# Convolution weights in two pools, the last stores of each convolution phase on ScalarE's queue, and the last two output tiles in pieces

## The chip, the cores and the metric

The kernel runs on one core of one Trainium2 chip. The metric is the device time of one execution in microseconds (us); the median of several runs counts. Single durations come from one profiled execution.

## The reference

The input x has 8 images of 256 channels of 56 x 56, float32. Two layers follow each other, each added to its own input:

```
x = x + involution(gn(x))          # layer 0: a 7x7 kernel per pixel and group, made from the pixel itself
x = x + tri_block(gn(x))           # layer 1

def tri_block(x):
    out1 = relu(batch_norm(conv3x3(x, ternary(w1))))
    out2 = batch_norm(conv3x3(out1, ternary(w2)))
    return relu(out1 + out2)
```

`gn` is a group norm. `ternary` turns a weight into -1, 0 or 1 by two thresholds, and the convolution counts its centre tap twice. `batch_norm` uses mean and variance over all 8 images, so nothing can be normalised until the last image's convolution is done.

## The kernel before

The work runs in four stages, one after the other, with all large intermediates in DRAM.

- **Layer 0** (to about 1180 us) computes the involution and stores its result x1 to DRAM (`x1_d`). It also turns the two weight tensors into ternary, transformed ones (`wq_d`). Its instructions are held in the order of the text by `pin`.
- **Phase 1** (`conv_phase(1, ...)`, to about 1615 us) computes the first convolution from x1 and stores its raw result to `y1_d`.
- **Phase 2** (`conv_phase(2, ...)`, to about 2060 us) normalises y1, applies Relu, computes the second convolution and stores its raw result to `y2_d`.
- **The final stage** (lines 1017 to 1037) reads y1, y2 and x1 again and writes relu(relu(bn(y1)) + bn(y2)) + x1.

A convolution phase loops over n = 0 to 15: an image b = n // 2 and its upper or lower half. The two-dimensional convolution is a one-dimensional transform along rows: `transform` makes six planes (k = 0 to 5) from four-row groups, each plane is multiplied by its own weights `wq[k]`, and the six products are combined to four rows. The planes are worked on in the order `ORDER = (1, 2, 3, 4, 0, 5)`, each with 24 matmuls (line 461), 12 for either half of the output channels. The input half n is loaded by `load` into two `raw` tiles (line 311), normalised into the padded buffer `xp`, and transformed through temporaries in the pool `tmpp` (tags `ta`, `tr`). VectorE writes the four rows of the result into `y`; the stores at line 501 wait for the last of them. ScalarE sums y and its square for the batch norm (line 416, with `dummy` as a place for the unused output); in the last half these sums are made in three parts as rows get ready (`last_rows`), and their results go through `batch_norm_params`, a chain of small VectorE instructions with one Sqrt on ScalarE. `weights(i, k)` loads one of the six weight tiles of 6144 bytes per partition; phase 1 gets all six before its loop, those of phase 2 follow in the last half of phase 1, each after the last matmul with its predecessor in the same place.

The final stage works on 16 tiles j (image b, half of the channels t), each of 128 partitions x 3136. For each it loads y1f, y2f and x1f on SP's queue (line 1026), and runs Relu on ScalarE (L1033), y2 times scale plus that on VectorE (L1034), Relu on ScalarE (L1035), and the addition of x1 on VectorE (L1036); ScalarE's queue stores the result (L1037). y1f_0 means the tile of y1 with j = 0. A name has two or three homes, and the load of y1f_2 waits until the home of y1f_0 is no longer read:

```
fa, fb, fc = ...                                     # three pools, one after the other in memory
homes = {"y1": (fc, fa), "y2": (fc, fb), "x1": (fc, fb, fb)}
```

The pools of the final stage lie where those of the convolution phases lay, in the same order from the start: `rawp` (12,992 bytes per partition), `wqp` (36,864), `pad` (14,848), `tmpp` (25,984), and others. `fa` (12,544) covers the raw tiles, `fb` (37,632) the end of the raw tiles, the weights and the first bytes of `pad`, and `fc` (37,632) covers `pad` and part of `tmpp`. A load may start when the last reader of what lay in its home's place is done.

Outside layer 0, the order of the instructions on each engine and queue is chosen when the kernel is built, by a planner: among the instructions that it takes for ready, the one that is earlier in the text goes first. On the chip, each queue is worked in that order, and an instruction that must wait holds up those behind it.

Of the kernel before, what the change touches and what calls it, by code (L numbers as in the profile page):

```python
# [8 lines left out]
F32 = mybir.dt.float32  # L9
F32R = mybir.dt.float32r  # L10
# [5 lines left out]
SBUF = bass.MemoryType.SB  # L16

P = 128
B, C, H, W = 8, 256, 56, 56
HW = H * W  # L20
CT = C // P
# [50 lines left out]
NH = HR * W  # L72
# [4 lines left out]
ORDER = (1, 2, 3, 4, 0, 5)  # L77
# [10 lines left out]
def involution_tri_block_kernel(  # L88
# [3 lines left out]
    nc = tc.nc  # L92
    out = out.rearrange("b c h w -> b c (h w)")
# [9 lines left out]
    x1_d, y1_d, y2_d = scratch("x1d"), scratch("y1d"), scratch("y2d")  # L103
# [191 lines left out]

    def weights(i, k):

        w = wqp.tile([P, CT, 3, C], F32R, tag=f"wq{k}", name=f"wq{i}_{k}")
        n = CT * 3 * C
        nc.sync.dma_start(w.rearrange("p t k o -> p (t k o)").bitcast(F32),  # L300
                          wq_d[i - 1][:, SLOT[k] * n:(SLOT[k] + 1) * n])
        return w

    def load(i, n, src_d):

        b, h = n // 2, n % 2
        raws = []
        for t in range(CT):
            raw = rawp.tile([P, RAW * W], F32, tag=f"raw{t}", name=f"raw{i}_{n}_{t}")
            r0 = h * (H - RAW)  # L310
            nc.sync.dma_start(raw, src_d[b][t][:, r0 * W:(r0 + RAW) * W])
            raws.append(raw)
        return raws

    def conv_phase(i, begun, src_d, norm, stats, shift, dst_d, follow):
# [6 lines left out]
        wq, raws = begun  # L322
# [104 lines left out]
        nxt, begun = {}, ({}, None)  # L427
        for _ in transform(0, raws, nxt):
            pass
        raws = load(i, 1, src_d)  # L430
        for n in range(2 * B):
            b, h = n // 2, n % 2
            cur, nxt = nxt, {}
            more = n + 1 < 2 * B
            steps = transform(n + 1, raws, nxt) if more else iter(())
            next(steps, None)
            final = n == 2 * B - 1
            if n + 2 < 2 * B:
                raws = load(i, n + 2, src_d)
            elif not final and follow:  # L440
                begun = {}, load(i + 1, 0, dst_d)
            y = wk.tile([P, CT, NH], F32, tag="y", bufs=2, name=f"y{i}_{n}")
            yr = [y.rearrange("p o (r k w) -> p o k r w", k=4, w=W)[:, :, k] for k in range(4)]

            def row_of(k, x, c, z, op):
                for to in range(CT):
                    nc.vector.scalar_tensor_tensor(yr[k][:, to], x[:, to], c, z[:, to],
                                                   ALU.mult, op)

            def half(name):  # L450
                return wk.tile([P, CT, HT, W], F32, tag=name, name=f"{name}{i}_{n}")

            m = {}
            for k in ORDER:
                ps = ps_c.tile([P, CT, 512], F32, tag="conv", name=f"c{i}_{n}_{k}")
                for to in range(CT):
                    c, last = 0, CT * 3 * 2 - 1
                    for part in cur[k]:
                        for t in range(CT):
                            for dx in range(3):  # L460
                                nc.tensor.matmul(  # L461
                                    ps[:, to, :NM], wq[k][:, t, dx, to * P:(to + 1) * P],
                                    part[:, t, :, dx:dx + W], start=(c == 0), stop=(c == last))
                                c += 1
                if final and follow:
                    begun[0][k] = weights(i + 1, k)
                m[k] = ps[:, :, :NM].rearrange("p o (r w) -> p o r w", w=W)
                next(done, None)
                if k in (2, 4):
                    e = half("e")  # L470
                    nc.scalar.copy(e, m[k])
                if k == 2:
                    s, d = half("s"), half("d")
                    nc.vector.tensor_tensor(s, m[1], e, ALU.add)
                    nc.vector.tensor_tensor(d, m[1], e, ALU.subtract)
                elif k == 4:

                    s2, d2 = half("s2"), half("d2")
                    nc.vector.tensor_tensor(s2, m[3], e, ALU.add)
                    nc.vector.tensor_tensor(d2, m[3], e, ALU.subtract)  # L480
                    nc.vector.tensor_tensor(yr[1], d2, d, ALU.subtract)  # L481
                    row_of(2, s2, 2.0, s, ALU.subtract)
                    for z, z2, c in ((s, s2, 0.5), (d, d2, 4.0)):
                        flat, flat2 = (v.rearrange("p o r w -> p (o r w)") for v in (z, z2))
                        nc.vector.scalar_tensor_tensor(flat, flat2, c, flat,
                                                       ALU.mult, ALU.subtract)
                    if final:
                        last_rows(n, y, 1, 2)
                elif k == 0:
                    row_of(0, m[0], 1.5, s, ALU.add)  # L490
                    if final:
                        last_rows(n + 1, y, 0, 1)
                elif k == 5:
                    row_of(3, m[5], 6.0, d, ALU.add)
                    if final:
                        last_rows(n + 2, y, 3, 1)
                next(steps, None)
            for _ in steps:
                pass
            for to in range(CT):  # L500
                nc.sync.dma_start(dst_d[b][to][:, h * NH:(h + 1) * NH], y[:, to])
            done = statistics(n, y)
        return begun

# [472 lines left out]


    with ExitStack() as ph2:
        rawp, wqp, pad, tmpp, planes, wk, ps_c = (  # L980
            ph2.enter_context(tc.tile_pool(name=name, bufs=bufs, space=space))
            for name, bufs, space in (
                ("rawp", 1, SBUF), ("wqp", 1, SBUF), ("pad", 1, SBUF), ("tmpp", 1, SBUF),
                ("planes", 8, SBUF), ("wk", 1, SBUF), ("ps_c", 4, PSUM)))

        def norm_x1(dst, src, b, t, engine):
            bias, scale = gn2[:, b, t, 1:2], gn2[:, b, t, 0:1]
            if engine is nc.scalar:
                nc.scalar.activation(dst, src, AF.Identity, bias=bias, scale=scale)
            else:  # L990
                nc.vector.tensor_scalar(dst, src, scale, bias, ALU.mult, ALU.add)

        begun = load(1, 0, x1_d)
        begun = {k: weights(1, k) for k in ORDER}, begun

        xp = pad.tile([P, 4, CT, HT + 1, WP], F32, tag="xp", name="xp")
        nc.gpsimd.memset(xp, 0.0)
        begun = conv_phase(1, begun, x1_d, norm_x1, st1, nc1, y1_d, True)

        sc1, bi1 = batch_norm_params(st1, nc1, g1_sb, b1_sb, "bn1")

        def norm_y1(dst, src, b, t, engine):
            bias, scale = bi1[:, t:t + 1], sc1[:, t:t + 1]
            if engine is nc.scalar:
                nc.scalar.activation(dst, src, AF.Relu, bias=bias, scale=scale)
            else:
                nc.vector.tensor_scalar(dst, src, scale, bias, ALU.mult, ALU.add)
                nc.vector.tensor_scalar(dst, dst, 0.0, None, ALU.max)  # L1010

        conv_phase(2, begun, y1_d, norm_y1, st2, nc2, y2_d, False)
# [3 lines left out]
    sc2, bi2 = batch_norm_params(st2, nc2, g2_sb, b2_sb, "bn2")  # L1016
    with ExitStack() as ph4:

        fa, fb, fc = (ph4.enter_context(tc.tile_pool(name=name, bufs=1))
                      for name in ("fa", "fb", "fc"))  # L1020
        homes = {"y1": (fc, fa), "y2": (fc, fb), "x1": (fc, fb, fb)}

        def loaded_image(name, j, src):
            k = j % len(homes[name])
            v = homes[name][k].tile([P, HW], F32, tag=f"{name}{k}", name=f"{name}f_{j}")
            nc.sync.dma_start(v, src)
            return v

        for b in range(B):
            for t in range(CT):  # L1030
                y1, y2, x1 = (loaded_image(name, b * CT + t, src[b][t])
                              for name, src in (("y1", y1_d), ("y2", y2_d), ("x1", x1_d)))
                nc.scalar.activation(y1, y1, AF.Relu, bias=bi1[:, t:t + 1], scale=sc1[:, t:t + 1])  # L1033
                nc.vector.scalar_tensor_tensor(y1, y2, sc2[:, t:t + 1], y1, ALU.mult, ALU.add)  # L1034
                nc.scalar.activation(y1, y1, AF.Relu, bias=bi2[:, t:t + 1])  # L1035
                nc.vector.tensor_tensor(x1, x1, y1, ALU.add)  # L1036
                nc.scalar.dma_start(out[b, t * P:(t + 1) * P, :], x1)  # L1037


# [69 lines left out]
```

## Time and profile before

| | us |
|---|---|
| median of 3 runs | 2310.3 |
| lowest and highest run | 2309.58, 2313.76 |
| the profiled execution | 2306.55 |
| its span, from first to last instruction | 2304.8 |

| engine | busy us | share of the span |
|---|---|---|
| PE (matmul) | 1872.9 | 81% |
| VectorE (DVE) | 1720.3 | 75% |
| ScalarE (ACT) | 1266.5 | 55% |
| GpSimd (POOL) | 589.4 | 26% |

The DMA engines moved 412.81 MB, 179 GB/s over the span. The busy shares are averages over stages with different limits, so they don't say what a change in one stage is worth; that is read from the stage itself. In the answers shown below, a timeline line has the start in us, the duration, the engine (SPq and ACTq are the DMA issues of SP and ScalarE), the line in the code, the operation, what is written from what, and how often; in square brackets stands how long the engine had been idle before, and which instruction ended that. A line of windows has the stretch and its length, then the busy time of PE, of PE's weight load, of DVE, ACT and POOL with the number of instructions in brackets, the granted PE clock, the busy share of the 16 DMA engines, and the GB/s that they moved.

### The profile page before, as it was taken

What the parts mean: (1) busy time and instruction counts of PE and PEld (TensorE: products, weight loads), DVE (VectorE), ACT (ScalarE), POOL (GpSimd) and SP (SyncE); (2) the same over time, 40 slices, a digit from 0 to 9 for tenths busy, and PEclk for the clock granted to TensorE, in tenths of its full rate; (3) what the DMA queues carried; (4) which work ended last, traced back from release to release, by engine and by line L of the source; (5) the groups of instructions that cost most, each with busy time, mean ns of one, the idle gap of its engine ahead of it and who ended that gap; (6) DMA issues with size and microseconds to landing.
All of it is one profiled execution on the core that took longest, in us unless ns stands there. A gap on an engine that the chain in (4) does not pass through costs nothing.

```text
span 2304.8 us, 72684 instructions
## 1 busy us (share of the span) xinstructions
PE 1872.9 (81%) x31088; PEld 1721.3 (75%) x31088; DVE 1720.3 (75%) x2898; ACT 1266.5 (55%) x2453; POOL 589.4 (26%) x1320
## 2 busy tenths in 40 slices
PE   5879888987988988999979999999799999970000
PEld 4767777776777777778779999999799999970000
DVE  3666867767677685765679999998899999964444
ACT  2545455455454555556546666665576666663433
POOL 3535555454454554646410000000000000000000
PEclk9989999999999999999989999999899999985555
DMA  4635657466465564735463333334333333359998
GB/s 156 198 106 175 190 143 211 145 183 189 118 202 160 173 202 137 212 118 166 138 235 114 114 115 130 139 131 154 122 137 126 114 114 114 130 222 398 426 430 377
DMA packets 159391, 412.81 MB, mean 179 GB/s; under 512 B 55518, under 2 KB 66140, under 8 KB 150876
## 3 DMA queue, kind: packets, MB, share of 16 engines
q1 hardware_dynamic: 154624, 381.35, 49.1%
q10 hardware_dynamic: 4444, 26.81, 2.8%
q8 instruction: 245, 4.01, 0.7%
q14 instruction: 78, 0.64, 0.1%
HBM read 264.05 MB, written 144.05 MB: 177 GB/s over the span
## 4 chain that ended last, share of the span: by engine, by line
PE 54%; DMA 9%; DVE 7%; ACT 3%; issue 2%; SPq 0%; POOL 0%; DVEq 0%; ACTq 0%; POOLq 0%
PE c L461 36%; PE pg L770 8%; PE pa L803 5%; DMA x1f<-x1d 4%; DMA y1f<-y1d 2%; PE ptq L737 2%; DVE a L779 2%; DMA out_y<-x1f 2%; PE pk L639 2%; PE pt L705 1%; DVE x1f L1036 1%; ACT a L774 1%; DVE inv L816 0%; DMA piece_w<-in_w 0%; DVE y1f L1034 0%
## 5 line engine op out<-in xcount | busy, mean ns | idle before, releaser
L461 PE MATMUL c<-pl,wq 128*128 128x392 f32 x4608 | 858.2, 348 | 22.0 <-ACT pl L351 20.3
L461 PEld LDWEIGHTS c<-pl,wq 128*128 128x128 f32 x4608 | 855.3, 190 | 24.7 <-ACT pl L351 20.7
L779 DVE TENSOR_TENSOR a<-pg,bt 126x756 f32<-126x756 f32 (+3 forms) x640 | 392.1, 654 | 182.2 <-ACT a L774 125.6
L770 PE MATMUL pg<-kr,wl 64*126 64x140 f32 (+1 forms) x6144 | 459.4, 293 | 53.7 <-DVE a L779 51.8
L770 PEld LDWEIGHTS pg<-kr,wl 64*126 64x126 f32 x6144 | 395.0, 195 | 107.8 <-issue 48.4
L803 PE MATMUL pa<-a,q 126*32 126x48 f32 x17920 | 276.0, 210 | 54.5 <-DVE a L779 28.7
L803 PEld LDWEIGHTS pa<-a,q 126*32 126x32 f32 x17920 | 227.0, 113 | 103.7 <-issue 34.8
L774 ACT ACTIVATE a<-pg,bt 126x126 f32<-126x126 f32 x768 | 244.0, 476 | 103.2 <-PE pg L770 103.2
L819 POOL TENSOR_TENSOR x<-x,inv 128x168 f32<-128x168 f32 x320 | 172.6, 540 | 472.7 <-DVE inv L816 394.1
L816 DVE SCALAR_TENSOR_TENSOR inv<-pa,half_sb,inv 128x168 f32<-128x168 f32 x320 | 117.0, 366 | 180.8 <-ACT inv L815 158.7
L351 ACT CAST pl<-r 128x812 fp32r<-128x812 f32 x192 | 162.4, 867 | 142.9 <-DVE r L346 126.7
L740 ACT COPY q<-ptq 126x384 f32<-126x384 f32 x320 | 139.2, 482 | 162.1 <-issue 89.8
L331 POOL MEMSET xp<- 128x116 f32 x32 | 6.3, 197 | 832.3 <-DVE a L346 832.3
L416 ACT ACTIVATE dummy<-y,nc 128x1568 f32<-128x1568 f32 (+2 forms) x144 | 210.1, 1459 | 5.3 <-DVE y L481 3.5
L352 DVE TENSOR_TENSOR pl<-r,pl 128x812 fp32r<-128x812 f32 x192 | 186.8, 999 | 29.9 <-ACT pl L351 28.8
L662 POOL TENSOR_SCALAR xn<-x,gn 128x224 f32<-128x224 f32 (+2 forms) x384 | 175.0, 476 | 117.7 <-PE pt L705 65.6
L662 POOL TENSOR_SCALAR xe<-x,gn 128x168 f32<-128x168 f32 (+2 forms) x384 | 164.8, 448 | 0.0
L737 PE MATMUL ptq<-ident_sb,xe 128*126 128x128 f32 x960 | 148.6, 292 | 1.8 <-issue 0.9
L708 ACT COPY stg<-pt 98x512 f32<-98x512 f32 x128 | 75.4, 589 | 132.6 <-issue 96.2
L149 DVE BATCH_NORM_STATS2 st<-x 128x6 f32<-128x392 f32 x256 | 138.0, 555 | 12.0 <-DMA x<-in_x 10.4
L815 ACT ACTIVATE inv<-pa,half_sb 128x168 f32<-128x168 f32 x320 | 128.5, 402 | 27.5 <-PE pa L803 24.8
L737 PEld LDWEIGHTS ptq<-ident_sb,xe 128*126 128x126 f32 x960 | 107.1, 145 | 16.8 <-issue 2.4
(144 smaller groups left out, 1826.3 us busy)
## 6 DMA issues: line engine op xcount, KB each, us to landing
q<-xtd SPq DMA_DIRECT2D x320, 252.0 KB
raw<-x1d SPq DMA_DIRECT2D x32, 812.0 KB
raw<-y1d SPq DMA_DIRECT2D x32, 812.0 KB
x<-in_x SPq DMA_DIRECT2D x64, 392.0 KB
xtd<-stg SPq DMA_DIRECT2D x128, 196.0 KB
x1d<-x SPq DMA_DIRECT2D x64, 392.0 KB
y1d<-y SPq DMA_DIRECT2D x32, 784.0 KB
y2d<-y SPq DMA_DIRECT2D x32, 784.0 KB
```

What stands on the lines that cost most here:

```text
L351: nc.scalar.copy(hi, r)
L352: nc.vector.tensor_tensor(lo, r, hi.bitcast(F32), ALU.subtract)
L416: nc.scalar.activation(dst, v, f, bias=shift[:, to:to + 1], accum_out=stats[:, to, j, n:n + 1])
L461: nc.tensor.matmul(ps[:, to, :NM], wq[k][:, t, dx, to * P:(to + 1) * P], part[:, t, :, dx:dx + W], start=(c == 0), stop=(c == last))
L662: nc.gpsimd.tensor_scalar(dst[:, i - d - k0:f - d - k0, :, x0:x0 + n], v[:, i:f, :, j0:j0 + n], scale, bias, ALU.mult, ALU.add)
L737: nc.tensor.transpose(pt[:NQ, k * P:(k + 1) * P], xe[c % 2][:, k, PY * ty:PY * ty + QY].rearrange("p r x -> p (r x)"), ident_sb)
L740: nc.scalar.copy(loads[b, c, ty][:NQ, NK:].rearrange("p k c -> p (k c)"), pt[:NQ, :NX * P])
L770: nc.tensor.matmul(dst, wl[rows, c, gp, o:o + NQ], kr[py][rows, px, :], start=True, stop=True)
L774: nc.scalar.activation(whole[:, g0 + i, p0 + j], ps[:NQ, i, j * nt:(j + 1) * nt], AF.Identity, bias=bt[:, c, g0 + i, p0 + j:p0 + j + 1])
L779: nc.vector.tensor_tensor(dst[:, g0:g0 + 2, p0:p0 + nv].rearrange("q g p t -> q g t p"), ps[:NQ, :, t0 * nv:t1 * nv].rearrange("q i (t p) ...
L803: nc.tensor.matmul(ps[o:o + 32, k * 2 * n:(k + 1) * 2 * n], q[:NQ, k, o:o + 32], av[:, t + k, g * 2 * n:(g + 1) * 2 * n], start=True, stop ...
L819: nc.gpsimd.tensor_tensor(xv, xv, iv.rearrange("p t (y x) -> p y t x", x=PX), ALU.add)
```

## The change

- The pool of the weights, `wqp`, becomes two: `wqa` for k = 1, 2, 3, 4 and `wqb` for k = 0, 5. A tile of 64 bytes per partition, `space`, is put ahead of the raw tiles, so that `wqa` ends at byte 37,632.
- Before the loop of phase 1 only the weights of k = 1, 2, 3 are asked for with the first raw tiles; those of 4, 0, 5 follow after the raw tiles of n = 1.
- In the last half of either phase (`final`), the two stores of y are issued on ScalarE's queue instead of SP's.
- The final stage has four pools: `fa` (12,544 bytes, over the raw tiles), `fb` (25,088, over the end of the raw tiles and `wqa`), `fc` (12,544, over `wqb` and the first bytes of `pad`), `fd` (37,632, at the addresses that `fc` had). y1f lives in fd and fa, y2f in fd and fb, x1f in fd, fb and fc.
- The last two tiles are loaded, computed and stored in pieces along the row: j = 14 in two, j = 15 in four.

```diff
     def weights(i, k):
-        w = wqp.tile([P, CT, 3, C], F32R, tag=f"wq{k}", name=f"wq{i}_{k}")
+        w = (wqb if k in ORDER[4:] else wqa).tile([P, CT, 3, C], F32R, tag=f"wq{k}",
+                                                  name=f"wq{i}_{k}")
...
         raws = load(i, 1, src_d)
+        for k in ORDER:
+            if k not in wq:
+                wq[k] = weights(i, k)
         for n in range(2 * B):
...
             for to in range(CT):
-                nc.sync.dma_start(dst_d[b][to][:, h * NH:(h + 1) * NH], y[:, to])
+                (nc.scalar if final else nc.sync).dma_start(
+                    dst_d[b][to][:, h * NH:(h + 1) * NH], y[:, to])
...
+        rawp.tile([P, 16], F32, tag="space", name="space")
         begun = load(1, 0, x1_d)
-        begun = {k: weights(1, k) for k in ORDER}, begun
+        begun = {k: weights(1, k) for k in ORDER[:3]}, begun
...
-        homes = {"y1": (fc, fa), "y2": (fc, fb), "x1": (fc, fb, fb)}
+        homes = {"y1": (fd, fa), "y2": (fd, fb), "x1": (fd, fb, fc)}
...
+        for j in range(B * CT):
+            b, t = j // CT, j % CT
+            y1f, y2f, x1f = (home(name, j) for name in ("y1", "y2", "x1"))
+            n = {B * CT - 2: 2, B * CT - 1: 4}.get(j, 1)
+            f = HW // n
+            for cols in (slice(k * f, (k + 1) * f) for k in range(n)):
+                y1, y2, x1 = y1f[:, cols], y2f[:, cols], x1f[:, cols]
+                for v, src in ((y1, y1_d), (y2, y2_d), (x1, x1_d)):
+                    nc.sync.dma_start(v, src[b][t][:, cols])
                 nc.scalar.activation(y1, y1, AF.Relu, bias=bi1[:, t:t + 1], scale=sc1[:, t:t + 1])
                 nc.vector.scalar_tensor_tensor(y1, y2, sc2[:, t:t + 1], y1, ALU.mult, ALU.add)
                 nc.scalar.activation(y1, y1, AF.Relu, bias=bi2[:, t:t + 1])
                 nc.vector.tensor_tensor(x1, x1, y1, ALU.add)
-                nc.scalar.dma_start(out[b, t * P:(t + 1) * P, :], x1)
+                nc.scalar.dma_start(out[b, t * P:(t + 1) * P, cols], x1)
```

More of the change, by code (lines that the diff above doesn't have):

```diff
@@ L979, in involution_tri_block_kernel @@
     with ExitStack() as ph2:
-        rawp, wqp, pad, tmpp, planes, wk, ps_c = (
+        rawp, wqa, wqb, pad, tmpp, planes, wk, ps_c = (
             ph2.enter_context(tc.tile_pool(name=name, bufs=bufs, space=space))
             for name, bufs, space in (
-                ("rawp", 1, SBUF), ("wqp", 1, SBUF), ("pad", 1, SBUF), ("tmpp", 1, SBUF),
+                ("rawp", 1, SBUF), ("wqa", 1, SBUF), ("wqb", 1, SBUF), ("pad", 1, SBUF),
+                ("tmpp", 1, SBUF),
                 ("planes", 8, SBUF), ("wk", 1, SBUF), ("ps_c", 4, PSUM)))
@@ L1017, in involution_tri_block_kernel, with home @@
     with ExitStack() as ph4:
-        fa, fb, fc = (ph4.enter_context(tc.tile_pool(name=name, bufs=1))
-                      for name in ("fa", "fb", "fc"))
-        homes = {"y1": (fc, fa), "y2": (fc, fb), "x1": (fc, fb, fb)}
-        def loaded_image(name, j, src):
+        fa, fb, fc, fd = (ph4.enter_context(tc.tile_pool(name=name, bufs=1))
+                          for name in ("fa", "fb", "fc", "fd"))
+        homes = {"y1": (fd, fa), "y2": (fd, fb), "x1": (fd, fb, fc)}
+        def home(name, j):
             k = j % len(homes[name])
[L1025 to L1032, printed above, removed]
+            return homes[name][k].tile([P, HW], F32, tag=f"{name}{k}", name=f"{name}f_{j}")
+        for j in range(B * CT):
[7 more added lines that the diff above has]
+                    nc.sync.dma_start(v, src[b][t][:, cols])
                 nc.scalar.activation(y1, y1, AF.Relu, bias=bi1[:, t:t + 1], scale=sc1[:, t:t + 1])
```

## The prediction

> **What bounds the kernel now.** I read the page's slices first, then the transfer rate window by window in the last stage, then SP's own queue, then the wait of each instruction around 2060 us.
>
> ```profile
> span 2304.8 us, 72684 instructions
> PE   5879888987988988999979999999799999970000
> DMA  4635657466465564735463333334333333359998
> ```
>
> A slice is 57.6 us. Through the two convolution phases (1183 to 2059 us) PE is the bound and the DMA engines are a third busy; in the last four slices PE is idle and the DMA engines are full. That is the final stage, lines 1017 to 1037. The change works on the seam between the two and on the end.
>
> ```profile
> 2055.50:2060.50 5.00, 3.35 (x19) 3.01 (x17) 2.88 (x5) 4.97 (x6) 0.00 (x0) 1.00 0.06 25
> 2060.50:2068.00 7.50, 0.00 (x0) 0.00 (x0) 0.72 (x5) 6.39 (x18) 0.00 (x0) 0.53 1.02 375
> 2076.00:2084.00 8.00, 0.00 (x0) 0.00 (x0) 6.82 (x2) 1.11 (x2) 0.00 (x0) 0.50 0.91 353
> 2112.00:2116.00 4.00, 0.00 (x0) 0.00 (x0) 3.63 (x2) 0.00 (x0) 0.00 (x0) 0.50 0.68 223
> 2144.00:2280.00 136.00, 0.00 (x0) 0.00 (x0) 62.20 (x18) 53.83 (x19) 0.00 (x0) 0.50 1.01 430
> 2294.20:2299.20 5.00, 0.00 (x0) 0.00 (x0) 3.43 (x1) 0.00 (x0) 0.00 (x0) 0.50 0.01 3
> ```
>
> The last two columns are the DMA share and GB/s. The steady rate is 430, so one image tile (128x3136 f32, 1.606 MB) costs 3.73 us and one j (three loads, one store) 14.9. The stage is worth attacking only where the rate is below 430. From 2055.5 to 2294.2 us the engines move 61 tiles (the last y2 store, 45 loads, 15 stores): 61 x 3.734 = 227.8 us in 238.7, so 10.9 us are lost. Each window's length times (1 - rate/430) says where: 4.7 in the gap at 2055.5, 1.0 to 2068, 1.4 in 2076 to 2084, 0.85 in 2092 to 2096 (339 GB/s), 1.9 at 2112, 0.6 in 2136 to 2144 (399), 0.4 at the end. A further 5.0 us is idle from 2294.2 to 2299.2, between the last load and the last store.
>
> ```profile
> 2042.26 0.80 SPq L501 DMA_DIRECT2D y2d<-y  x2
> 2043.84 0.32 SPq L1026 DMA_DIRECT2D y1f<-y1d  x1
> 2044.21 1.26 SPq L1026 DMA_DIRECT2D y2f<-y2d  x1
> 2059.48 0.80 SPq L501 DMA_DIRECT2D y2d<-y  x2
> 2060.32 0.92 SPq L1026 DMA_DIRECT2D x1f<-x1d  x1
> 2061.34 1.20 SPq L1026 DMA_DIRECT2D y2f<-y2d  x1
> 2062.58 1.12 SPq L1026 DMA_DIRECT2D x1f<-x1d  x1
> 2073.25 0.32 SPq L1026 DMA_DIRECT2D y2f<-y2d  x1
> 2079.72 0.32 SPq L1026 DMA_DIRECT2D y1f<-y1d  x1
> 2080.08 0.43 SPq L1026 DMA_DIRECT2D x1f<-x1d  x1
> ```
>
> With a y1f issued at 2020.13, three of the first six tiles already load ahead. SP then stands at the y2 stores until 2059.48, when VectorE has made the last row, and x1f_0, y2f_1, x1f_1 queue behind them. That is the 4.7 us gap.
>
> ```profile
> 2067.18 0.23 DVE L176 TENSOR_REDUCE bmv_bn<-st 128x4 f32<-128x72 f32 x1 [7.25 <-ACT dummy L416]
> 2069.74 3.48 DVE L1034 SCALAR_TENSOR_TENSOR y1f<-y2f,sc_bn,y1f 128x3136 f32<-128x3136 f32 x1
> ```
>
> This is the wait that takes over if loads come earlier: ScalarE's statistics end at 2067.2, the batch-norm scale is there at 2069.7, and no home is freed before that. The first (of y2f_0) is free at 2073.2, the next (of y1f_0) at 2079.7.
>
> **What the Trainium skill says.** DMA: Bandwidth & Descriptors, section Issuing engines are not separate DMA queues: DMAs from SP and ScalarE share the same 16 engines; a second queue saves only issue time. The trace agrees: SP's loads and ScalarE's stores together move 430 GB/s. So the stores' new queue gives no bandwidth, only SP's freedom. Section Where 436 GB/s comes from: a ceiling of 435; steady 430 agrees, so nothing is to be had inside the full windows. Section Anatomy of one DMA: about 2 us fixed per DMA, mostly completion. Here the last load's data end at 2294.2 and VectorE starts at 2295.22; the last store is issued at 2298.68, its data take 3.8 us, the span ends at 2304.8. Same page, Specifications: rows of 512 B or more run at line rate; the smallest new row is 3136 B.
>
> **The change part by part.** (a) *Last stores to ScalarE's queue.* In phase 2, SP no longer waits for the last row: x1f_0 follows y2f_0, its data from 2055.5. ScalarE issues two stores of some 0.35 us each (row out_y: 338 to 365 ns). Behind them on ScalarE stand statistics, Sqrt of the batch norm, Relus. Between: at best 0, placed after the last statistic, where ScalarE waits 1.1 us for VectorE; at worst ahead of the statistics (rival 4). The same happens at the seam of the phases near 1615, where PE waits 16 us for this chain; I take one store there on the chain, 0.35. In phase 2 such a delay is covered by transfers still running.
>
> (b) *Two weight pools.* fb now lies over rawp's end and wqa (k = 1 to 4), fc over wqb (k = 0, 5). wqa is free when the k = 4 matmuls end, 2050.0 (ScalarE's copy of it starts there), so y2f_1 and x1f_1 are in time for their turns at 2059 and 2063. fd has the addresses fc had, so y1f_0, y2f_0, x1f_0 are freed as before at 2043.8. Matmuls do not suffer: in the 4 us windows from 2044 to 2056 with a DMA share of 0.8 to 1.02, PE does 23 to 24 matmuls, as with none.
>
> (c) *The seventh tile.* What SP issues after x1f_1 is fixed when the kernel is built: by text order among what the planner takes for ready. Before, it chose y2f_2, though y1f_2 comes first in the text: the plan had the first L1034 done by then and not the first L1036, two steps (2.9 + 3.4 us here) later. It did not choose x1f_2, whose home was free. Without the y2 stores (1.6 MB) SP's plan reaches that point a tile earlier, likely ahead of the first L1034, and only x1f_2 is ready. So I take x1f_2 as seventh, free at 2058.5.
>
> (d) *The sum at the seam.* From 2055.5: x1f_0, y2f_1, x1f_1, x1f_2 and the y2 store, 5 x 3.73 plus the 1.0 of the mixed window: busy to 2075.2. y2f_2 is freed at 2073.2 to 2073.6: no gap, busy to 2078.9. y1f_2 and the first output wait for L1036, 2079.7 to 2080.2 (the second L1034 may now go before it), data 0.6 later: a gap of 1.7. Tile j=1 is finished near 2083.6, not 2089.5, so I drop the dip at 2112 and keep 1.9 for the other late losses. Lost after: 1.0 + 1.7 + 1.9 = 4.6, against 10.9: **6.3 gained**.
>
> (e) *Pieces.* The last quarter needs, after its load's data end: y2 ended 1.2 earlier, landing 1.1, L1034 0.97 (rows of 812: 1.00), Relu 0.85 (784 copied: 0.81), add 0.97, three hops of 0.1, issue and start 0.5: the store's data begin 3.5 later, instead of 5.0. If the third quarter's store is still to go, 2.5 of idling. Gain 1.5 to 2.5; **2.0**. The other quarters' stores move ahead of that load, so nothing more is gained. Twelve more loads in all cost SP 0.4 us each, while it waits anyway. Shorter rows: y stores (6272 B) ran 1.61 MB in 3.9 us, 410 GB/s; x loads at the start (3136 B) 370 in the window 12 to 16. At 370 the last j would cost 2.1 more, at 430 nothing: **0.5 lost**.
>
> (f) *Weights at the start of phase 1.* The first three before raw n=1, the others after. The first matmul (1182.8) waits for pl, not weights; k = 4 is needed at 1196.3, while wq was issued by 1181.3, and raw n=1 is first read at 1195.45 behind other ScalarE work. If SP stands at raw n=1 first, it waits for raw n=0 to be read (the last read, by VectorE, ends at 1177.9) with the three weights behind it: a delay of 10 us is covered, and if the order went badly it costs at most the 1 to 2 us by which k = 4 would slip. Taken 0. The 64 B space tile costs nothing.
>
> Sum: 6.3 + 2.0 - 0.5 - 0.35 = 7.45. The profiled execution took 2306.55 (span 2304.8), so 2299.1; it lies 3.75 below the median 2310.3, and against that the forecast is **2302.9**.
>
> **The rivals.** 1. *Six tiles only*, y2f_2 seventh as before. Busy to 2071.4, gaps of 2.6 and 2.8: lost 8.3, gain at the seam 2.6, in all 3.75: 2306.5. For it: that order is in the present queue. 2. *y1f_2 heads SP's queue*: nothing loads from 2071.4 to 2080.5; lost 12.0, the head start becomes a wait, and the pieces pay it back: 2310.3. The same if loads do not start ahead at all. 3. *All full*: the later losses vanish and y1f_2's gap is filled: 12 gained, 2298. 4. *Slower: ScalarE's in-order queue.* If the y store stands ahead of the 12 statistics, ScalarE waits for the last row. At the first seam they run 1609.4 to 1619.7; after a row ready at 1615.2 and 0.7 of issue they end at 1626.2: 6.5 lost. At the second they end 3.7 later and the gaps grow to rival 1's: in all 2.7 slower, 2313.0, or 6 with rival 2's order. It decides once about five statistics stand behind the store. Against it: they come first in the text.
>
> **How the numbers follow.** Forecast 0.56, rival 1 0.20, rival 2 0.10, rival 3 0.07, rival 4 0.07. 0.2% is 4.6 us, about what a measurement of this kernel can tell from no change. Faster: most of the forecast, a third of rival 1, rival 3: 0.68. Within: 0.26. Slower: 0.06. The range from 2298 (rival 3) to 2310 (short of rivals 2 and 4) leaves out about a fifth, and takes in the bounds of (a), (e), (f).
>
> **What would show it.** In the changed profile: x1f_0 issued near 2045.5, y2f_1 and x1f_1 right after 2050, x1f_2 next; DMA share near 1 from 2055 to 2079; the statistics still ending by 2067.6, at the first seam by 1620.1; no dip near 2112; 3.5 us or less between last load and last store. If SP waits in front of a free home, or ScalarE's statistics end over 2 us later, the forecast is wrong.

## The result, and the profile after

| | before | changed |
|---|---|---|
| median of 9 runs each, us | 2306.98 (2298.77 to 2313.76) | 2296.48 (2288.67 to 2301.02) |
| the profiled execution, us | 2306.55 | 2293.04 |
| its span, us | 2304.8 | 2291.3 |

The ratio of the two is 0.995, with an interval of 0.9931 to 0.9969: the changed kernel is faster, by half a per cent. A second set, the changed kernel again beside the one before on another occasion, gave 0.9968 (0.9955 to 0.9981). The direction is that of the forecast; its time, 2302.9 us, is 6.4 above the median measured, which lies just below the range of 2298 to 2310.

To see where the time went, I cut each profiled execution at four instructions: the first matmul of phase 1, VectorE's start on the last row of y in phase 1, the first matmul of phase 2, and the start on the last row in phase 2. I call the parts layer 0, phase 1, seam, phase 2 and last stage (this last one begins some 8 us before the statistics end, while ScalarE still works on y2).

| us | layer 0 | phase 1 | seam | phase 2 | last stage |
|---|---|---|---|---|---|
| before | 1182.84 | 431.30 | 15.97 | 428.78 | 245.91 |
| changed | 1178.73 | 428.96 | 15.96 | 428.43 | 239.22 |
| difference | -4.1 | -2.3 | 0.0 | -0.35 | -6.7 |

The page of the changed kernel, its slices:

```profile
span 2291.3 us, 72716 instructions
PE   5879888887888989999979999999799999980000
DMA  4635647565375564745563333333333333369999
```

The last stage is still one in which the DMA engines are full and PE is idle. What changed is seen in the rate by windows. The first window below corresponds to the gap before the change (25 GB/s for 5 us), the second to the one at 375, the third to the one at 353; the row at 2104 corresponds to the dip at 223.

```profile
2048.70:2053.70 5.00, 3.34 (x18) 3.00 (x17) 2.87 (x5) 4.97 (x6) 0.00 (x0) 1.00 1.02 434
2053.70:2061.20 7.50, 0.00 (x0) 0.00 (x0) 0.73 (x5) 6.38 (x18) 0.00 (x0) 0.73 1.00 398
2069.20:2077.20 8.00, 0.00 (x0) 0.00 (x0) 7.34 (x3) 3.12 (x2) 0.00 (x0) 0.50 0.95 365
...
2104.00:2108.00 4.00, 0.00 (x0) 0.00 (x0) 2.18 (x1) 0.00 (x0) 0.00 (x0) 0.50 0.74 281
2132.00:2136.00 4.00, 0.00 (x0) 0.00 (x0) 3.53 (x2) 0.00 (x0) 0.00 (x0) 0.50 0.74 235
2144.00:2240.00 96.00, 0.00 (x0) 0.00 (x0) 44.94 (x13) 39.77 (x14) 0.00 (x0) 0.50 1.01 427
2287.00:2289.00 2.00, 0.00 (x0) 0.00 (x0) 0.90 (x1) 0.00 (x0) 0.00 (x0) 0.50 0.46 179
```

The gap is filled. But there are now two dips later on, at 2104 and at 2132, where the forecast had one smaller sum of "late losses". At the end, some 2 us at less than half the rate stand where 5.0 us stood idle.

SP's own queue in the changed kernel, as a timeline:

```profile
2035.43 0.80 SPq L505 DMA_DIRECT2D y2d<-y  x2
...
2038.69 0.87 SPq L1044 DMA_DIRECT2D x1f<-x1d  x1
2043.18 0.32 SPq L1044 DMA_DIRECT2D y2f<-y2d  x1
2043.54 8.85 SPq L1044 DMA_DIRECT2D x1f<-x1d  x2
2066.43 3.79 SPq L1044 DMA_DIRECT2D y2f<-y2d  x2
2073.23 3.65 SPq L1044 DMA_DIRECT2D y1f<-y1d  x2
```

The last pair of y2 stores is gone from this queue, and x1f_0, y2f_1, x1f_1 and x1f_2 go out between 2038.7 and 2052.4, before or with the last row (which VectorE starts at 2052.1). Then come y2f_2 and y2f_3 together, and y1f_2 and y1f_3 together. All engines, the same kernel's timeline around the end of the statistics:

```profile
2060.37 0.23 DVE L176 TENSOR_REDUCE bmv_bn<-st 128x4 f32<-128x72 f32 x1 [7.25 <-ACT dummy L417]
2062.92 3.48 DVE L1046 SCALAR_TENSOR_TENSOR y1f<-y2f,sc_bn,y1f 128x3136 f32<-128x3136 f32 x1
```

VectorE's first work after the statistics stands 8.3 us after the start of the last row, as before (2067.18 against 2058.89), and its idle time in brackets is the same 7.25. The stores on ScalarE's queue delayed no statistic.

### The profile page after: what moved, and what is told of

Read it like the earlier page. It is cut to its first block, busy times and chain, and to the rows that moved or that the text cites. A ratio compares the mean times of both kernels' runs of the same rounds, so it can differ in the third digit from the quotient of the medians.

```text
span 2291.3 us, 72716 instructions
## 1 busy us (share of the span) xinstructions
PE 1861.3 (81%) x31088; PEld 1711.4 (75%) x31088; DVE 1721.1 (75%) x2906; ACT 1267.5 (55%) x2461; POOL 586.5 (26%) x1320
```

## The experiments

Each was profiled once. A time of a single run says little here, since layer 0 alone moves by several us from execution to execution; the conclusions rest on the segments. Their own scatter shows where the same instructions ran again: the last stage took 245.91 and 246.77 us (before and e3), and 239.22, 239.08 and 239.40 (changed, e6 and e11), so a difference below 0.9 decides nothing there. All of them together:

| us | layer 0 | phase 1 | seam | phase 2 | last stage |
|---|---|---|---|---|---|
| before | 1182.84 | 431.30 | 15.97 | 428.78 | 245.91 |
| e1_stores | 1191.90 | 431.81 | 15.96 | 429.07 | 243.46 |
| e2_pieces | 1186.37 | 430.92 | 15.96 | 428.52 | 242.53 |
| e3_raw_first | 1188.91 | 428.92 | 15.97 | 428.43 | 246.77 |
| e4_pools | 1183.80 | 431.79 | 15.97 | 429.08 | 245.86 |
| e8_stores_pools | 1184.04 | 431.42 | 15.95 | 428.81 | 242.68 |
| changed | 1178.73 | 428.96 | 15.96 | 428.43 | 239.22 |
| e5_no_pieces | 1186.69 | 428.47 | 15.96 | 428.19 | 242.79 |
| e6_weights_first | 1191.87 | 431.99 | 15.96 | 429.20 | 239.08 |
| e11_changed_again | 1186.04 | 428.22 | 15.96 | 429.48 | 239.40 |
| e9_x1_home | 1186.49 | 428.30 | 15.95 | 429.56 | 239.50 |
| e7_more_homes | 1179.43 | 429.37 | 15.96 | 428.72 | 232.92 |
| e10_y_homes | 1185.31 | 429.23 | 15.95 | 428.62 | 232.89 |
| e12_y_homes_timed | 1192.72 | 429.25 | 15.98 | 428.60 | 232.95 |

**One part alone, added to the kernel before: e1 to e4.** The first is only the stores on ScalarE's queue:

```diff
-                nc.sync.dma_start(dst_d[b][to][:, h * NH:(h + 1) * NH], y[:, to])
+                (nc.scalar if final else nc.sync).dma_start(
+                    dst_d[b][to][:, h * NH:(h + 1) * NH], y[:, to])
```

> Only the stores of the last y on ScalarE's queue; pools, homes, weights and pieces as before. Last stage (from VectorE's last row of y to the end): 245.9 us before, 239.2 after the whole change. My theory: SP's freedom is what fills the gap, and the two pools add little, since the transfers of x1f_0 last until the weights are free anyway: 240.5 to 242. Rival (the two pools are needed for tiles to load ahead): 244 or more. Both: phase 1 stays at 431.3 us (from its first matmul to its last row), the seam between the phases at 16.0.

2314.01 us, beside 2310.49 for the kernel before; the longer time is layer 0's (+9.1). The last stage is 2.45 shorter, 243.46, which is neither the 240.5 to 242 that I had expected nor the rival's 244 or more. It still has a gap, in the window at the last row:

```profile
2068.74:2072.74 4.00, 0.00 (x0) 0.00 (x0) 1.04 (x2) 3.87 (x10) 0.00 (x0) 0.81 0.77 216
```

With the old homes y2f_1 is issued only at 2068.73, after the last matmuls, and x1f_1 behind it. So freeing SP alone is worth 2.45 and leaves some 2 us of the gap.

The second is only the pieces of the last two tiles, in the old homes:

```diff
+            n = {B * CT - 2: 2, B * CT - 1: 4}.get(j, 1)
+            f = HW // n
+            for cols in (slice(k * f, (k + 1) * f) for k in range(n)):
...
```

> Only the last two tiles in pieces, all else as before. My theory (the last store's data begin sooner after the last load): last stage 243.4 to 244.4 instead of 245.9, that is 1.5 to 2.5 less. Rival (short rows and more transfers eat it up): 245.5 or more. Phase 1 stays at 431.3.

2306.07 beside 2310.49; the last stage is 3.4 shorter, more than the 1.5 to 2.5 expected before this run and the 2.0 - 0.5 = 1.5 of the prediction's (e).

The third is only the order of the loads at the start of phase 1:

```diff
-        begun = {k: weights(1, k) for k in ORDER}, begun
+        begun = {k: weights(1, k) for k in ORDER[:3]}, begun
...
         raws = load(i, 1, src_d)
+        for k in ORDER:
+            if k not in wq:
+                wq[k] = weights(i, k)
```

> Only the order of the first loads of phase 1: three weights, raw n=1, three weights; all else as before. The changed kernel's phase 1 is 429.0 us against 431.3, which the prediction had not seen. Theory A (the earlier raw n=1 lets ScalarE normalise it some 8 us sooner, so half n=1 starts without waiting): phase 1 is 429.0 here too. Rival B (the shorter phase 1 comes from the layout or from the stores on ScalarE's queue at its end): 431.3. The last stage stays at 245.9.

2310.75 beside 2310.49, with layer 0 6.1 longer. Phase 1 is 2.4 shorter, 428.92, and everything behind it is unchanged within 0.9. So the part that the prediction took at nothing carries the whole gain of phase 1.

The fourth is only the two pools and the homes that follow from them:

```diff
...
-        homes = {"y1": (fc, fa), "y2": (fc, fb), "x1": (fc, fb, fb)}
+        homes = {"y1": (fd, fa), "y2": (fd, fb), "x1": (fd, fb, fc)}
```

> Only the two weight pools and the homes of the changed kernel; stores on SP's queue, weights in the old order, no pieces. My theory: SP still stands at the stores with x1f_0 behind them, so the free homes are of no use: last stage 245.4 to 246.4. Rival (earlier free homes are the gain): 243 or less.

2308.37 beside 2310.49; no segment after layer 0 differs from before by more than 0.5. So an earlier home alone was worth nothing here, where SP stands at the y2 stores ahead of the load.

**Two parts together: e8.** Stores and pools, neither pieces nor the new order of loads. Edit, against the changed kernel:

```diff
-        for k in ORDER:
-            if k not in wq:
-                wq[k] = weights(i, k)
...
-        begun = {k: weights(1, k) for k in ORDER[:3]}, begun
+        begun = {k: weights(1, k) for k in ORDER}, begun
...
-            n = {B * CT - 2: 2, B * CT - 1: 4}.get(j, 1)
+            n = 1
```

> Stores on ScalarE's queue and the two pools, without pieces and with the old order of the first loads. Stores alone took 2.4 us from the last stage, pools alone nothing. Theory A (with SP free, the pools close the gap at the last row, where the rate was 216 GB/s for 4 us in the run with the stores alone): last stage 242.0 to 243.0. Rival B (pools add nothing): 243.5. Phase 1 as before, 431.3.

2304.68, one run, beside a median of 2312.68 in 16 runs of the kernel before. The last stage is 242.68: the two parts together gain 3.2, the 2.45 of the stores and 0.8 more. In the window where e1 had 216 GB/s there is no gap now:

```profile
2060.22:2064.22 4.00, 0.00 (x0) 0.00 (x0) 1.03 (x2) 3.87 (x10) 0.00 (x0) 0.78 1.03 408
```

So the homes do close what e1 left of the gap, 1.8 us of full rate in this window. Only 0.8 of that, no more than the scatter, arrives at the end of the stage. The 3.2 is what came of the head of the last stage, for which the prediction's (d) had 6.3.

**Parts taken out of the changed kernel: e5 and e6.** Without the pieces:

```diff
-            n = {B * CT - 2: 2, B * CT - 1: 4}.get(j, 1)
+            n = 1
```

> The changed kernel without the pieces (each of the 16 tiles whole). The pieces alone took 3.4 us from the last stage (245.9 to 242.5) where the prediction had 1.5. Theory A (the gain is that idle DMA engines at the end are filled, whatever went before): 242.6 here, 3.4 more than the changed kernel's 239.2. Rival B (pieces and head start share a gain): 241 or less.

2303.85 us. The last stage is 242.79, 3.6 longer than with the pieces. The pieces' gain thus measured 3.4 in the kernel before and 3.6 in the changed one.

With all six weights ahead of the raw tiles again:

```diff
-        for k in ORDER:
-            if k not in wq:
-                wq[k] = weights(i, k)
...
-        begun = {k: weights(1, k) for k in ORDER[:3]}, begun
+        begun = {k: weights(1, k) for k in ORDER}, begun
```

> The changed kernel with all six weight loads of phase 1 ahead of raw n=1 again. Theory A: phase 1 takes 431.3 us as before the change, not 429.0, and the last stage stays at 239.2. Rival B (the pools or ScalarE's stores shorten phase 1): 429.0.

2309.9 us, of which layer 0 has 1191.87. Phase 1 is back at 431.99, and the last stage stays short at 239.08: the two gains are independent. What PE waited for in phase 1 shows where the time goes. The columns are the engine and line that waits, what it waits for, the total in us, how often, and the longest. First the kernel before, from its first matmul to its last row, then the changed one, then e6 without its first wait, 4.5 us for pl:

```profile
PE c L461 <- ACT pl L351: 4.2, 1, 4.2
PE c L461 <- ACT e L471: 0.9, 1, 0.9
PE c L461 <- DVE d L475: 0.7, 1, 0.7
```

```profile
PE c L465 <- ACT pl L352: 4.2, 1, 4.2
```

```profile
PE c L462 <- ACT e L472: 0.9, 1, 0.9
PE c L462 <- DVE d L476: 0.7, 1, 0.7
```

The wait for pl is the one before the very first matmul. The other two, at 1221 and 1236 in the kernel before, exist only where all six weights go first. They make 1.6 of the 2.3; the rest is not put down to a wait by the trace.

**What makes the dips: e7, e9, e10.** Behind the head of the last stage the changed kernel runs at 364, 281 GB/s from 2100 to 2108 and at 342, 235, 411 from 2128 to 2140; at 430 these stretches would be 4.8 us shorter. SP's waits in the window 2120 to 2134 of the changed kernel say which instruction held the home that the next load needed. The first line is the wait of the y1f issued at 2132.22, the second that of the y2f issued at 2120.26:

```profile
SPq L1044 <- DVE x1f L1048: 11.6, 1, 11.6
SPq L1044 <- DVE y1f L1046: 5.3, 1, 5.3
```

L1048 is the last reader of a y1f, L1046 of a y2f. Both dips begin while SP waits for a y1f's home, until 2102.87 and until 2132.22. The first of the three kernels gives a fifth pool, at addresses behind the others, to all three names:

```diff
...
-        homes = {"y1": (fd, fa), "y2": (fd, fb), "x1": (fd, fb, fc)}
+        homes = {"y1": (fd, fa, fe), "y2": (fd, fb, fe), "x1": (fd, fb, fc, fe)}
```

> The changed kernel with a fifth pool of 37,632 bytes behind the others: a third home for y1f and y2f, a fourth for x1f, so tile j=2 too can load ahead, freed by the last matmul. In the changed kernel the rate falls to 281 GB/s 52 to 56 us after the last row and to 238 at 80 to 84: two tiles finish together, and the next loads wait for the same additions and stores. Theory A (these dips are waits for homes): they vanish, and the last stage takes 233 to 236 us instead of 239.2; in all 0.991 to 0.994 of the kernel before. Rival B (mixing of loads and stores, or HBM, makes the dips): 238.5 to 240.

2295.89 in the median of 11 runs, ratio to before 0.9945 (0.9922 to 0.9968). The last stage is 232.92, 6.3 shorter than in the changed kernel. More homes take away the limit behind the head. Which of them, the next two tell apart. The fifth pool for x1f alone:

```diff
...
-        homes = {"y1": (fd, fa), "y2": (fd, fb), "x1": (fd, fb, fc)}
+        homes = {"y1": (fd, fa), "y2": (fd, fb), "x1": (fd, fb, fc, fe)}
```

> The changed kernel with a fourth home for x1f alone (y1f and y2f keep two). With third homes for y too the dips went and the last stage took 232.9 us instead of 239.2. Theory A (SP stands at x1f_3 until output 0 has landed, with y2f_4 and y1f_4 behind it; the x1 home is the bottleneck): most of the gain comes here, 233 to 235. Rival B (the additions that free y1f's home set the pace): 237.5 or more.

2301.59 beside 2309.4; the last stage is 239.50, no shorter, and both dips are there, in its windows:

```profile
2112.30:2116.30 4.00, 0.00 (x0) 0.00 (x0) 2.23 (x1) 0.00 (x0) 0.00 (x0) 0.50 0.81 278
2140.30:2144.30 4.00, 0.00 (x0) 0.00 (x0) 3.46 (x2) 0.00 (x0) 0.00 (x0) 0.50 0.76 235
```

I had held x1f's home for the bottleneck; that theory fell. The fifth pool for y1f and y2f alone:

```diff
...
-        homes = {"y1": (fd, fa), "y2": (fd, fb), "x1": (fd, fb, fc)}
+        homes = {"y1": (fd, fa, fe), "y2": (fd, fb, fe), "x1": (fd, fb, fc)}
```

> The changed kernel with third homes for y1f and y2f, x1f keeping three. Theory A (x1f's home is the bottleneck): 237.5 or more for the last stage. Rival B (y's homes, above all y1f's, set the pace): 233 to 235, nearly the 232.9 of both together.

2293.79 beside 2309.4; the last stage is 232.89, and the places of the two dips run at the full rate in its windows:

```profile
2107.60:2119.60 12.00, 0.00 (x0) 0.00 (x0) 5.78 (x2) 8.06 (x3) 0.00 (x0) 0.50 1.00 427
2135.60:2147.60 12.00, 0.00 (x0) 0.00 (x0) 5.25 (x2) 3.29 (x2) 0.00 (x0) 0.50 1.00 429
```

So the dips are waits for the homes of y1f and y2f; a third home for one of them alone was not tried. The 6.3 us are not the dips alone: with these homes y1f_2 and y2f_2 load at the last row (issued at 2059.11 and 2059.47), and by the rates from 9 to 33 us behind the last row about 1.2 of the 6.3 is won there.

**The changed kernel again, and the better version, timed: e11 and e12.** e11 is the changed kernel, unaltered; e12 is e10, timed. Both ran on the same chip, beside 26 runs of the kernel before (median 2309.68).

> The changed kernel once more, unaltered. The first profile's layer 0 took 1178.7 us, but the ten kernels so far, all with the same instructions there, took 1178.7 to 1191.9, longer with more time at half TensorE clock. Theory A (layer 0 is scatter, the change is worth 2.3 in phase 1 and 6.7 in the last stage): phase 1 428.3 to 429.4 and last stage 238.6 to 239.8 again, layer 0 anywhere from 1178 to 1192; median ratio 0.996, that is 9.0 us. Rival B (the change shortens layer 0 by 4 us): layer 0 below 1181 again, ratio 0.994.

2301.39 in the median of 21 runs, ratio 0.9968 (0.9955 to 0.9981). Layer 0 took 1186.04 in its profile, 7.3 more than in the first profile of the same kernel; phase 1 and the last stage are the same (428.22 and 239.40).

> The changed kernel with third homes for y1f and y2f, timed beside the changed kernel on one chip. By the profiles 6.8 us less in the last stage (232.4 against 239.2): a ratio 0.003 below that of the changed kernel, 0.993 of the kernel before. If the time does not follow the stage, the ratios are equal within 0.001.

2297.18 in the median of 6 runs, ratio 0.9938 (0.9917 to 0.9958). The last stage is again 232.95. The two intervals of e11 and e12 just overlap, so by the runs alone its lead of 0.0030, or 6.9 us, isn't certain; the last stages, 6.1 to 6.6 us shorter in each of the three kernels that have the homes than in the four without them that are otherwise alike (changed, e6, e9, e11), say that it is there. e12 is the better version.

## Why the prediction was right and wrong

The seven kernels of this list with the new order of loads and the changed one itself have a phase 1 of 428.2 to 429.4, mean 428.84; the five with all weights first and the kernel before have 430.9 to 432.0, mean 431.54. The last stage has 246.2 in the mean of the kernel before, e3 and e4, and 239.3 in that of the changed kernel, e6, e9 and e11. So the change removes 2.7 + 6.9 = 9.6 us, a ratio of 0.9958, which lies in both measured intervals. The prediction's sum was 7.45. By its steps:

**(a), the stores: right, and cheaper than forecast.** The one store taken on the chain at the first seam, 0.35, wasn't paid: the seam is 15.96 against 15.97. In the trace of the changed kernel ScalarE issues the stores at 1608.29 and 1608.82 while its statistics run on one after the other without a gap (1608.01, 1608.75, 1609.50), so an issue lies beside a running ACTIVATE. By the Trainium skill, DMA: Bandwidth & Descriptors, section Issuing engines are not separate DMA queues, a second queue brings no bandwidth and saves only the issuing engine's time. The traces agree on the bandwidth (430 GB/s before, 427 in the changed kernel), and the issues, 0.33 to 0.34 us each, cost ScalarE nothing that the seam shows. **Rival 4**, ScalarE's queue blocked ahead of the statistics, did not come: the stores stand among them, but no statistic waits for them longer than before.

**(b), matmuls beside loads: right.** PE did 18 matmuls in 3.34 us at 434 GB/s, where it had done 19 in 3.35 us at 25; phase 2 has the same length in all kernels within 1.4 us, whichever parts they have.

**(c), the seventh tile: right.** x1f_2 followed x1f_1 on SP's queue, and was issued at 2052.07, 0.01 ahead of the last row, where the prediction had its home free 0.4 ahead of it. Rivals 1 and 2 fell with that.

**(d), the sum at the seam: this step failed, in one term.** The issue times it predicted came to within a few tenths: x1f_0 near 2045.5 of the old clock is 13.4 before the last row, and measured 2038.69 is too; y2f_2 at 2073.2 to 2073.6 is 14.3 to 14.7 after it, measured 14.4; y1f_2 at 20.8 to 21.3, measured 21.2. The gaps of 1.0 and 1.7 around these are there as well: the rates of 398 in the second window and 365 in the third make 0.6 and 1.2. The term that was mis-sized is the last, "the other late losses", taken at 1.9 with the dip at 2112 dropped. Measured are 4.8. My argument was that tile j = 1 would finish earlier, and it did. But the dip stayed, some 50 us behind the last row (at 2104 now), and a second one came at 2132. Each begins where two tiles finish as a pair, as at 2112 in the kernel before (L1036 x2 at 2108.88). VectorE in the changed kernel:

```profile
2099.42 6.75 DVE L1048 TENSOR_TENSOR x1f<-x1f,y1f 128x3136 f32<-128x3136 f32 x2
```

On VectorE the L1046 of the second tile of a pair stands ahead of the L1048 of the first, so that neither of y1f's two homes comes free before the first of these two L1048 ends. With the earlier loads the pairs begin with tiles 0 and 1 (L1048 x2 at 2069.79, y2f_2 and y2f_3 issued in one stretch, y1f_2 and y1f_3 too), where the kernel before still finished these two one by one. e10 shows that a third home for y1f and y2f takes both dips away; whether finishing tile by tile in the old homes would, was not tried. So of 6.3 forecast 3.2 came (e8). The two gaps at the head, 0.9 smaller than forecast, and the dips, 2.9 larger, account for 2.0 of the missing 3.1; the rest is spread over stretches a little below 430, such as the 427 from 2144 to 2240 (0.7).

**(e), the pieces: right in kind, too low.** 3.4 to 3.6 against 1.5. The tail of the changed kernel, ScalarE's issues of the last stores:

```profile
2283.84 1.44 ACTq L1049 DMA_DIRECT2D out_y<-x1f  x2
...
2287.93 0.34 ACTq L1049 DMA_DIRECT2D out_y<-x1f  x1
```

The prediction let 2.5 to 3.5 us of idling stand between the last load and the last store, because it had the other quarters' stores go out ahead of that load. They did not: the first was issued at 2280.82, behind a Relu on ScalarE's queue that waited 3.74 us for its own load, and the next two from 2283.84 on, all after the last load was issued at 2278.13. So they moved with it and behind it and filled part of the wait for the last quarter: the 2 us at 179 GB/s that the window above shows are 1.2 us lost. From 5.0 to 1.2 is 3.8, and the shorter rows, at 410 GB/s in the 5 us from 2282 to 2287, cost 0.2 there; that gives the 3.6 of the changed kernel. The prediction had allowed for one of these stores, the third quarter's (its 2.5), and not for three.

**(f), the order of loads in phase 1: this step failed too.** Taken at 0, measured at 2.7. The prediction saw raw n=1 first read at 1195.45 "behind other ScalarE work" and took that work for cover. That was a wrong reading of the trace: the load was not covered, it had only just come. By their loads' semaphores the two raw tiles of n=1 landed at 1193.95 and 1195.90, behind the weights. With the tiles asked for ahead of three weights, they landed at 1182.47 and 1184.45 in the changed kernel, and ScalarE normalises them sooner. First the kernel before, then the changed one:

```profile
1195.45 5.05 ACT L989 ACTIVATE xp<-raw,gn 128x392 f32<-128x392 f32 x8
```

```profile
1185.87 0.76 ACT L995 ACTIVATE xp<-raw,gn 128x448 f32<-128x448 f32 x1 [0.95 <-DVE a L347]
```

That is 7.1 us after the first matmul instead of 12.6, and the two stops of PE, 38 and 53 us after it in the kernel before, are gone. The other ScalarE work stood first in an order made when the kernel is built; that the planner put it there because it held the tile for late fits this, but its plan is not on record. The prediction weighed what the new order could cost, and not what it could gain.

**The sum and its level.** Three terms came out better than forecast, (f) by 2.7, (e) by 1.9 to 2.1 and (a) by 0.35, and (d) by 3.1 worse: 7.45 became 9.6, which is 2.2 of the 6.4 us between forecast and measured median. So what took the time below the forecast's range is (f), (e) and the level, not (d); that (d)'s miss hid more than half of the others was luck. Another 3.3 of the 6.4 us is the anchor: the median of the first 3 runs of the kernel before, 2310.3, against which the forecast was set, came out at 2306.98 over 9 runs (and at 2312.68 and 2309.68 in the later sets of 16 and 26). The last 0.9 is the difference between the two medians, 10.5 apart, and the segments' 9.6. I had bounded every edit and not the median that they were subtracted from; two medians that each move by some us make a range of 12 us too narrow on that count alone. The measured median lies nearest to rival 3's 2298, but not for its reason: rival 3 had the later losses vanish, and they grew.

On the profiled execution the forecast was 2299.1 and 2293.04 was measured. Of these 6.1, 4.1 is layer 0, in which the change alters only the order of the last loads: its instructions are the same on every engine. e11 decided that it is scatter: the same kernel had 7.3 more there.

## What to carry to other kernels

When a load looks covered by work that runs ahead of its first use, look when it lands; landing just before that use, it was not covered, and moving it earlier can be worth something (2.7 us here). When a gap at the head of a stage is filled, count the homes per name for the steady part behind it: here two homes that were freed as a pair gave part of the gap back as dips, and a third home brought 6.1 to 6.6 us, about twice the 3.2 of the head start. And compare segments between the same instructions, since the parts before the change can scatter by more than the change is worth.

## What had not been expected of the hardware

Layer 0, with the same instructions in all kernels, took 1178.7 to 1192.7 us in 14 profiles, 0.6% of the whole time from end to end. The profiles come from several chips, but the four of e1 to e4, from one chip, alone span 1183.8 to 1191.9. By the trace's clock records TensorE was granted half its clock for 77 to 118 us of layer 0, and the longer times tend to go with more of that (84 us with 1178.73, 118 us with 1192.72; but 108 us with both 1182.84 and 1188.91, and 77 us, the least, with 1185.31). What sets the clock, and whether it makes layer 0 longer, was not tried.

In the two convolution phases, where PE is busy throughout, the records do account for the scatter. TensorE had half its clock there for 2.8 to 6.0 us in a phase. Taking half of that time off, as if an us at half clock did half its work, phase 2 is 426.5 to 426.8 in all 14 profiles instead of 428.2 to 429.6, and phase 1 is 429.0 to 429.2 with all weights first and 426.5 to 426.8 with the new order. So the order of the loads is worth 2.4 to 2.5 us at full clock, and the remaining 0.2 to 0.3 of the 2.7 above is the clock.
